# A graph message layer on one core: one of 124 edge groups is summed from SBUF instead of being scattered

## The chip, the cores and the metric

The kernel runs on one core of a Trainium2 chip. The metric is the time of one execution on the device in microseconds (us). A core has TensorE (PE, matmuls, with weight loads shown apart as PEld), VectorE (DVE), ScalarE (ACT), GpSimd (POOL) and SyncE (SP), each with its own instruction stream, and 16 DMA engines that all of them start transfers on. SBUF is the on-chip memory with 128 partitions, PSUM the memory that matmuls write to.

## The reference

There are 6250 nodes with 64 features and 206250 edges, sorted in the reference by destination. For each edge the features of one end (`col`) and the 64 edge attributes go through a layer with ReLU; the results are averaged over the edges of each node (`row`); two more layers, a residual and a layer norm follow per node. Everything is fp32.

```python
msg = jnp.concatenate([src_node_features[col], edge_attr], axis=1)
h = jax.nn.relu(msg @ W1a.T + b1a)          # 206250 x 128
h = h @ W1b.T + b1b
sums = jax.ops.segment_sum(h, row, num_segments=n_nodes)
counts = jax.ops.segment_sum(ones, row, num_segments=n_nodes)
agg = sums / jnp.maximum(counts, 1.0)[:, None]
z = jax.nn.relu(jnp.concatenate([x, agg], axis=1) @ W2a.T + b2a)
z = z @ W2b.T + b2b
out = layernorm(x + jnp.concatenate([z, x], axis=1) @ Wr.T + br)
```

The node that an edge is summed into (`row`, called src in the kernel) is random over all nodes; the node that it reads (`col`, dst in the kernel) rises along the list of edges.

## The kernel before

**Tiles, groups, bins.** Edges are padded to 206336 = 1612 tiles of 128. 13 tiles are a group (1664 edges); the 124 groups are taken in an order shuffled by a fixed step. Nodes are cut into 49 bins of 128. The second layer of the messages is applied after the mean, so what is summed per edge is the ReLU output, 128 numbers and a one for the count.

**Scatter and sum.** Edges of one bin lie anywhere in the list. So the kernel sorts rows by bin through DRAM: each group's 1664 rows (128 numbers, the one, and the node's place in its bin: 520 bytes) are written by 13 indirect DMAs on POOL, 128 rows each, to the next free slots of their bins (L959). Later the rows of a bin are read back in tiles of 128 (L1008, SP), DVE compares the place of each row with a ramp 0 to 127 to make a one-hot matrix per tile (L1037), and PE multiplies one-hot and rows, so that the rows of each node are added in PSUM (L1053). DVE adds the result into `part`, an SBUF array of all bins (L1109).

**Epochs and steps.** The groups are split in five epochs (`EPOCHS`, 82, 17, 14, 7 and 4 groups) that use three DRAM buffers in turn. Epoch 0 is read in steps: once 4, 8, 12, 16 and 18 tiles of every bin are surely full (`FULL`), those are read while later groups are still scattered; the last step of an epoch reads the rest up to a bound that no bin exceeds. A step's sums come in groups of up to 3 bins and 14 tiles ("sum groups"), spread evenly over the iterations of the next step and begun 4 iterations late (`LATE`). Nine buffers hold rows that were read (`READS`).

**The loop.** One iteration k handles group k (L1179 to L1263). In program order it

- starts the loads of group k+3 (`group`, L899): edge attributes into the upper half of an `rhs` buffer (L697, 416 KB), the places of the read nodes in a window of 64 nodes into its lower half (L914), and the 64 rows of the node table of that window into `mv` (L920). There are four `rhs` buffers (`EDGES`), so L697 waits until the matmuls of group k-1 have read theirs;
- counts bins for group k+1 on PE (`counts_of`, L852 and L853);
- computes the hidden layer of group k for tiles 0 to 9 (`hidden`, 128x128x128 matmuls at L952 in three parts; ACT applies the ReLU into an `orow` buffer, L953);
- makes the one-hot columns of group k+2 on DVE (`columns`, L932: 64x1664, in place over the places loaded by L914) and its bins and running counts (`bins_of`, L832, L833 and the scan L839);
- issues reads of rows for due sum groups as buffers are free (`issue`);
- does the due sum groups: `sum_next` runs the matmuls of one, makes the one-hots of the next (`mark`) and collects the one before. After the first, `slots` makes the row addresses of group k+1 (L869, L874). After the second (or after the only one), the last hidden part of group k is computed (tiles 10 to 12), and the scatter of group k is issued; a third sum group comes behind it.

The order on PE, ACT, DVE and SP is the order of the program (`manual_schedule`); an instruction that waits holds those behind it on its engine. POOL's scatters run in program order too; the eleventh of a group needs the ReLU of the last hidden part.

After the loop the last sums are done bin by bin together with the node layers and the layer norm (the tail). If the input doesn't fit the kernel's assumptions, a slower path is taken; it is not taken here.

Of the kernel before, what the change touches and what calls it, by code (L numbers as in the profile page):

```python
# [451 lines left out]
EPOCHS = (82, 17, 14, 7, 4)  # L452
# [4 lines left out]
BIG = 2.0**20  # L457
LATE = 4
# [5 lines left out]
ROWS, EDGES, READS = 5, 4, 9  # L464
# [13 lines left out]
def fast_path(  # L478
# [40 lines left out]
    NGR = NT // NG  # L519
    REM = N - (NB - 1) * P  # L520
# [6 lines left out]
    assert NT % NG == 0 and NGR == sum(EPOCHS) and HEAD % BLK == 0 and sorted(order) == list(range(NGR))  # L527
# [100 lines left out]
    mvs = const.tile([P, MV, H], F32, name="mv")  # L628
    nc.scalar.dma_start(mvs[:D], w1aT[D:, None, :].to_broadcast([D, MV, H]))
    mv = [mvs[:, i, :] for i in range(MV)]  # L630
# [45 lines left out]
    with (  # L676
# [17 lines left out]


        def edges(g):
            nc.sync.dma_start(rhss[g % EDGES][:D, :], edgeT[:, g * NG * P : (g + 1) * NG * P])  # L697
# [201 lines left out]
        def group(g):  # L899

            rhs = rhss[g % EDGES]
            if g < NEAR:
                all_of = dst[g * NG * P : (g + 1) * NG * P].rearrange("(o e) -> o e", o=1)
                s = nc.sync.dma_start(rhs[D:, :].bitcast(I32), all_of.to_broadcast([WIN, NG * P]))
                edges(g)
                with tc.issue_after(s.ins):
                    w = nc.sync.value_load(win_i[0:1, g : g + 1], min_val=0, max_val=N - WIN)
                nc.sync.dma_start(near[:D, g, :], xT[:, bass.ds(w, WIN)])
                return rhs, None, mv[g % MV]
            edges(g)  # L910

            half = NG * P // 2
            rel = rhs[D:, :].bitcast(BF16).rearrange("p (h e) -> p h e", h=2)[:, :, half:]
            s = nc.sync.dma_start(  # L914
                rel, relt[g : g + 1, :].rearrange("o (h e) -> o h e", h=2).to_broadcast([WIN, 2, half])
            )
            with tc.issue_after(s.ins):
                w = nc.sync.value_load(win_i[0:1, g : g + 1], min_val=0, max_val=N - WIN)
            m = mv[g % MV]
            nc.sync.dma_start(m[D:, :], ytab[bass.ds(w, WIN), :])  # L920
            return rhs, rel, m
# [23 lines left out]
        def hidden(k, parts):  # L945
            orow = orows[k % ROWS]
# [136 lines left out]

        class Sums:
# [6 lines left out]

        issued, marked, totals = [], [], []

        def mark():

            if issued:
                g = issued.pop(0)
                g.oh = nodes_of(g.st, g.reads)
                marked.append(g)
# [11 lines left out]
        def sum_next():  # L1111
# [5 lines left out]
            summed(g.st, g.reads, g.oh, lambda b: g.ps[:, b - g.b0, :])  # L1117
# [7 lines left out]
        groups_at = [[] for _ in range(NGR + LATE)]  # L1125
        for st, after in zip(steps, steps[1:]):
            grs = groups_of(st)
            n = after.at - st.at
            for i in range(n):
                groups_at[st.at + LATE + i] = [(st, g) for g in grs[i * len(grs) // n : (i + 1) * len(grs) // n]]  # L1130
        to_issue = []

        def issue(k):

            while to_issue and sum(len(g.reads) for g in issued + marked) + len(to_issue[0][1]) <= READS:
                issued.append(Sums(k, *to_issue.pop(0)))
# [42 lines left out]
        for k, ep_ in enumerate(epoch_of):  # L1179

            if k + 3 < NGR:
                made[k + 3] = group(k + 3)
# [8 lines left out]
            if k + 1 < NGR:  # L1191
# [9 lines left out]
            if k + 2 < NGR:  # L1201
# [19 lines left out]
            if k == 4:  # L1221
# [17 lines left out]
                nc.vector.tensor_add(wrx_t[:D, :], wrx_t[:D, :], ident[:D, :D])  # L1239
            if 0 <= k - PRE < -(-NB // SUB):  # L1240
# [5 lines left out]
            for i in range(max(due, 1)):  # L1246
# [3 lines left out]
                if i == 0 and k + 1 < NGR:  # L1250
                    slots(k + 1, counts)
                if i == min(1, max(due, 1) - 1):
                    if k > 0:
                        hidden(k, ((10, 3),))
                    made.pop(k)
                    scatter(ep_, k)
# [7 lines left out]
        for k in range(NGR, NGR + LATE):  # L1264
# [10 lines left out]
        with tc.tile_pool(name="nw", bufs=3) as nw:  # L1275
# [68 lines left out]
            for i in range(n_last + 5):  # L1344
                issue(NGR)
# [4 lines left out]
                issue(NGR)  # L1350
# [85 lines left out]
```

## Time and profile before

| | |
|---|---|
| median of 3 runs | 2570.15 us (2557.39 to 2579.05) |
| profiled execution | 2561.73 us, span 2559.9 us |
| granted TensorE clock, mean | 0.715 |
| busy: PE, PEld, DVE, ACT, POOL | 57%, 50%, 46%, 13%, 60% |
| scatters (L959) | 1612 of 958 ns, first at 14.6, last ends at 2434 |
| hidden matmuls (L952) | 3224 records, 642.8 us busy |
| sum matmuls (L1053) | 4006 records, 614.2 us busy |
| edge loads (L697, L914, L920) | 124 groups, 416 KB + 208 KB + window |

The profile is of one execution, by the hardware's profiler. An fp32 matmul leaves two records, so 2003 tiles were summed. "Idle before" an instruction is the time its engine stood still, with what ended it: "DMA rhs<-relt" is the landing of that transfer, "issue" means that the engine waited for nothing the profile shows, "remote" that the event came from a core or queue that the profile doesn't know. SPq and POOLq are instructions by which an engine starts a transfer. Groups are numbered in the order in which they are handled; "block k" are the 13 scatters of group k.

### The profile page before, as it was taken

Reading aid. Unit: us, or ns where it says so; the run is one execution under the profiler, and the core shown is the slowest. Engines: PE = TensorE matmul, PEld = TensorE weight load, DVE = VectorE, ACT = ScalarE, POOL = GpSimd, SP = SyncE. Lnnn points to the kernel's source line nnn. Section 1 sums busy time; section 2 is a strip of 40 time slices with the busy share of each in tenths; the row PEclk is TensorE's granted clock in tenths of the full one; section 3 lists DMA queues with packets and bytes.
Section 4 is the critical chain, followed back from the end, with each engine's and each line's share of the span. In section 5 each row is a group of like instructions: output and inputs, shape, how many; then the busy total and the mean of one; then the engine's idle time right before and its main releaser. Section 6 shows DMA issues by size and latency. Waiting matters only on the chain. (4 is left out here: it accounts for less than half of the span.)

```text
span 2559.9 us, 25031 instructions
## 1 busy us (share of the span) xinstructions
PE 1455.2 (57%) x8253; PEld 1270.7 (50%) x8253; DVE 1184.9 (46%) x1993; ACT 326.1 (13%) x807; POOL 1547.4 (60%) x1629
## 2 busy tenths in 40 slices
PE   4555543345555554545655566665666665666796
PEld 3444442344444444434544455555555564566695
DVE  5233334233343443533444345465555454555587
ACT  1111111111111010101101011111001010100106
POOL 5566666666666666666666665656666666666600
PEclk7656666666776776767676677776776776777899
DMA  7467635544434444434444455644545554555581
GB/s 163 142 224 239 194 116 165 179 116 116 135 115 122 133 120 120 127 106 134 123 133 119 128 153 150 170 131 142 155 139 153 154 145 148 158 167 171 162 258 38
DMA packets 198839, 375.23 MB, mean 147 GB/s; under 512 B 47105, under 2 KB 114036, under 8 KB 198572
## 3 DMA queue, kind: packets, MB, share of 16 engines
q1 hardware_dynamic: 121370, 223.70, 31.7%
q0 software_dynamic: 51584, 107.40, 13.2%
q10 hardware_dynamic: 25746, 42.45, 5.0%
q8 instruction: 67, 1.10, 0.2%
q14 instruction: 72, 0.59, 0.1%
HBM read 221.77 MB, written 151.59 MB: 146 GB/s over the span
## 5 line engine op out<-in xcount | busy, mean ns | idle before, releaser
L959 POOL DMA_INDIRECT rows<-orow,rowidx x1612 | 1544.9, 958 | 886.2 <-issue 472.9
L952 PE MATMUL h_ps<-mv,rhs 128*128 128x128 f32 x3224 | 642.8, 351 | 457.0 <-issue 313.5
L952 PEld LDWEIGHTS h_ps<-mv,rhs 128*128 128x128 f32 x3224 | 579.0, 260 | 532.9 <-issue 371.1
L1053 PE MATMUL sum_ps<-rt,oh 128*128 128x129 f32 x4006 | 614.2, 309 | 266.2 <-issue 224.9
L1053 PEld LDWEIGHTS sum_ps<-rt,oh 128*128 128x128 f32 x4006 | 572.7, 223 | 295.1 <-issue 249.4
L953 ACT ACTIVATE orow<-h_ps 128x512 f32<-128x512 f32 x496 | 247.8, 518 | 2046.4 <-remote 1228.3
L1037 DVE TENSOR_TENSOR oh<-ramp,rt 128x512 f32<-128x512 f32 (+3 forms) x213 | 145.6, 703 | 562.4 <-DMA rt<-rows 361.9
L932 DVE TENSOR_TENSOR rhs<-rhs,ramp 64x1664 f32<-64x1664 bf16 x116 | 219.5, 1892 | 30.4 <-DMA rhs<-relt 16.8
L1109 DVE TENSOR_TENSOR part<-part,sum_ps 128x258 f32<-128x258 f32 (+2 forms) x183 | 86.2, 472 | 273.5 <-remote 186.1
L839 DVE TENSOR_TENSOR_SCAN had<-ramp,bins 128x700 bf16<-128x700 bf16 x124 | 200.3, 1615 | 4.2
L852 PE MATMUL cnt_ps<-had,one_w 128*128 128x350 bf16 x248 | 101.4, 411 | 176.6 <-issue 101.3
L1037 DVE TENSOR_TENSOR oh<-ramp,node 128x512 f32<-128x512 f32 (+3 forms) x237 | 187.4, 791 | 8.0
L869 DVE TENSOR_REDUCE row<-cnt_ps 128x14 f32<-128x700 f32 x124 | 109.1, 880 | 52.4 <-PE cnt_ps L853 24.3
L853 PEld LDWEIGHTS <-before_w 128*128 128x128 bf16 x248 | 28.9, 117 | 201.1 <-issue 188.9
L1034 DVE SCALAR_TENSOR_TENSOR node<-unused,rt 128x4 f32<-128x4 bf16 (+3 forms) x237 | 37.9, 160 | 195.1 <-DMA rt<-rows 118.4
L853 PE MATMUL cnt_ps<-bins,before_w 128*128 128x325 bf16 x248 | 103.2, 419 | 31.2 <-issue 31.2
L833 DVE TENSOR_TENSOR bins<-ramp,hi 128x650 bf16<-128x650 f32 x124 | 108.2, 873 | 0.0
L1158 DVE TENSOR_SCALAR zT<-h_ps 128x512 f32<-128x512 f32 (+1 forms) x13 | 8.6, 661 | 140.3 <-remote 73.0
L852 PEld LDWEIGHTS <-one_w 128*128 128x128 bf16 x248 | 30.6, 123 | 59.9 <-issue 49.3
L1153 PE MATMUL h_ps<-zT,w2x_t 65*128 65x512 f32 (+1 forms) x26 | 22.2, 952 | 57.8 <-ACT orow L953 55.9
L1162 PE MATMUL h_ps<-nwzz_t,zT 128*128 128x64 f32 x98 | 22.3, 402 | 46.1 <-DVE zT L1158 43.2
L832 DVE TENSOR_TENSOR bins<-had,ramp 128x50 bf16<-128x50 bf16 x119 | 44.1, 370 | 2.7
(112 smaller groups left out, 390.9 us busy)
## 6 DMA issues: line engine op xcount, KB each, us to landing
rt<-rows SPq DMA_DIRECT2D x242, 260.0 KB
rhs<-in_edgeT SPq DMA_DIRECT2D x124, 416.0 KB
rt<-rows SPq DMA_DIRECT2D x106, 390.0 KB
rows<-orow,rowidx POOLq DMA_INDIRECT x1612
rhs<-relt SPq DMA_DIRECT2D x116, 208.0 KB
rows<-padrow ACTq DMA_DIRECT2D x4, 4680.0 KB
rows<-padrow ACTq DMA_DIRECT2D x8, 2340.0 KB
rt<-rows SPq DMA_DIRECT2D x48, 325.0 KB
```

The costliest lines, as they stand in the source:

```text
L833: nc.vector.tensor_tensor(by_bin[:, :, 1:], ramp[:, : 2 * HALF, None].to_broadcast([P, 2 * HALF, BLK]), hi[:, None, c0 : c0 + BLK].to_broa ...
L839: nc.vector.tensor_tensor_scan(had, on, oh, 0.0, op0=ALU.mult, op1=ALU.add)
L852: nc.tensor.matmul(v, one_w, had[:, b, :], start=True, stop=False)
L853: nc.tensor.matmul(v[:, :, :BLK], before_w, oh[:, b, 1:], start=False, stop=True)
L869: nc.vector.tensor_reduce(row, v.rearrange("p i b t -> p t i b"), axis=mybir.AxisListType.XY, op=ALU.max)
L932: nc.vector.tensor_tensor(rhs[D:, :].rearrange("p (h e) -> p h e", h=2), rel, in_win[D:, :, None].to_broadcast([WIN, 2, NG * P // 2]), op= ...
L952: nc.tensor.matmul(ps[:, j, :], rhs[:, c * P : (c + 1) * P], m, start=True, stop=True)
L953: nc.scalar.activation(orow[:, k0 : k0 + n, :H], ps[:, :n, :], AF.Relu)
L959: s = nc.gpsimd.indirect_dma_start(out=ep_.rows, out_offset=bass.IndirectOffsetOnAxis(ap=rowidx[:, t : t + 1], axis=0), in_=orow[:, j, :], ...
L1037: nc.vector.tensor_tensor(res[:, at_tile : at_tile + nb * n, :], ramp[:, None, :].to_broadcast([P, nb * n, P]), node[:, :, None].to_broadc ...
L1053: nc.tensor.matmul(of_bin(b), oh[:, at_tile, :], rt[:, j * n + t, : H + 1], start=t0 + t == st.lo[b], stop=t0 + t == st.hi[b] - 1,)
L1109: nc.vector.tensor_add(to, to, g.ps[:, : g.nb, :])
```

## The change

Group 123, the last, isn't scattered any more (`WHOLE = 1`); the loop runs over 123 groups (`NSC`) and the first epoch has 81. Group 123 is loaded at k = 10 into space lent from the read buffers and a fifth `mv` buffer, its columns are made at k = 13 and its hidden layer at k = 14, into an SBUF buffer of its own (`wrow`, 128x13x129). It is then summed bin by bin: each of 49 items subtracts 128 b from the node numbers, makes a one-hot of all 13 tiles for bin b in one operation (rows of other bins get none), multiplies the 13 tiles and adds the result into `part`. The items stand among the other sum groups in iterations 40 to 116.

The edge buffers (`rhs`) are three instead of four. Because the load of group k+3 then overwrites the buffer of group k, its issue moves from the start of iteration k to behind the last hidden part of group k.

With 81 groups in epoch 0, the bound on a bin's tiles is 24, not 25: the last step of the epoch reads 6 tiles of each bin (one read) where it read 7 (two reads of 4 and 3).

```diff
--- before.py
+++ after.py
@@ -449,19 +449,21 @@
 NG = 13
 WIN = 64
 STEP = 77
-EPOCHS = (82, 17, 14, 7, 4)
+EPOCHS = (81, 17, 14, 7, 4)
 NEAR = 8
 Y_AHEAD = 32
 HEAD = 117
 FULL = (4, 8, 12, 16, 18)
 BIG = 2.0**20
+WHOLE = 1
+WHOLE_AT = 10
 LATE = 4
 BUFS = 3
 RD = 6
 SUMS, TILES = 3, 14
 SEG = 9
 PRE = 6
-ROWS, EDGES, READS = 5, 4, 9
+ROWS, EDGES, READS = 5, 3, 9
 SPREAD = 4.8
 EARLY = 14
 CLEAR = 4
@@ -517,6 +519,7 @@
     E = NT * P
     NB = N // P + 1
     NGR = NT // NG
+    NSC = NGR - WHOLE
     REM = N - (NB - 1) * P
     NE = len(EPOCHS)
     W = H + 2
@@ -524,7 +527,7 @@
     HALF = -(-NB // 2)
     T = BLK + 1
     order = order_of(NGR)
-    assert NT % NG == 0 and NGR == sum(EPOCHS) and HEAD % BLK == 0 and sorted(order) == list(range(NGR))
+    assert NT % NG == 0 and NGR == sum(EPOCHS) + WHOLE and HEAD % BLK == 0 and sorted(order) == list(range(NGR))
 
     class Epoch:
         pass
@@ -625,9 +628,9 @@
     nc.scalar.dma_start(w1x_t[:D, :], w1aT[:D])
     nc.scalar.dma_start(w1x_t[D:, :], b1a.rearrange("(o p) -> o p", o=1))
     MV = 4
-    mvs = const.tile([P, MV, H], F32, name="mv")
-    nc.scalar.dma_start(mvs[:D], w1aT[D:, None, :].to_broadcast([D, MV, H]))
-    mv = [mvs[:, i, :] for i in range(MV)]
+    mvs = const.tile([P, MV + 1, H], F32, name="mv")
+    nc.scalar.dma_start(mvs[:D], w1aT[D:, None, :].to_broadcast([D, MV + 1, H]))
+    mv = [mvs[:, i, :] for i in range(MV + 1)]
     zT = const.tile([P, NB * P], F32, name="zT")
 
     near = lent(2 * NT + NG * P * 3 // 2, NEAR * WIN).rearrange("p (g w) -> p g w", w=WIN)
@@ -692,9 +695,16 @@
             nc.gpsimd.memset(r[:, :, H], 1.0)
         rhss = [rp.tile([P, NG * P], F32, name=f"rhs{i}") for i in range(EDGES)]
 
+        def rhs_of(g):
+            return rhss[g % EDGES] if g < NSC else lent(0, NG * P)
+
+
+        wrows = [op.tile([P, BLK, H + 1], F32, name=f"wrow{i}") for i in range(WHOLE)]
+        for r in wrows:
+            nc.gpsimd.memset(r[:, :, H], 1.0)
 
         def edges(g):
-            nc.sync.dma_start(rhss[g % EDGES][:D, :], edgeT[:, g * NG * P : (g + 1) * NG * P])
+            nc.sync.dma_start(rhs_of(g)[:D, :], edgeT[:, g * NG * P : (g + 1) * NG * P])
 
         dst_i = lent(2 * NT, NG * P)[:NGR].bitcast(I32)
         rel = lent(2 * NT + NG * P, NG * P // 2)[:NGR].bitcast(BF16)
@@ -898,7 +908,7 @@
 
         def group(g):
 
-            rhs = rhss[g % EDGES]
+            rhs = rhs_of(g)
             if g < NEAR:
                 all_of = dst[g * NG * P : (g + 1) * NG * P].rearrange("(o e) -> o e", o=1)
                 s = nc.sync.dma_start(rhs[D:, :].bitcast(I32), all_of.to_broadcast([WIN, NG * P]))
@@ -916,7 +926,7 @@
             )
             with tc.issue_after(s.ins):
                 w = nc.sync.value_load(win_i[0:1, g : g + 1], min_val=0, max_val=N - WIN)
-            m = mv[g % MV]
+            m = mv[g % MV if g < NSC else MV]
             nc.sync.dma_start(m[D:, :], ytab[bass.ds(w, WIN), :])
             return rhs, rel, m
 
@@ -943,7 +953,7 @@
         made = {}
 
         def hidden(k, parts):
-            orow = orows[k % ROWS]
+            orow = orows[k % ROWS] if k < NSC else wrows[k - NSC]
             rhs, _, m = made[k]
             for k0, n in parts:
                 ps = hp.tile([P, SUB, H], F32, name="h_ps")
@@ -1081,6 +1091,32 @@
                 res[-1].append((b, nb, t0, n))
             return res
 
+        class Whole:
+
+
+            def __init__(self, i, b):
+                self.st, self.reads, self.i, self.b0, self.nb = None, [], i, b, 1
+
+            def one_hots(self):
+                node = nodep.tile([P, BLK], F32, name="node_w")
+                nc.vector.tensor_scalar(node, wsrc[self.i], float(self.b0 * P), None, op0=ALU.subtract)
+                res = ohp.tile([P, TILES, P], F32, name="oh")
+                nc.vector.tensor_tensor(
+                    res[:, :BLK, :],
+                    ramp[:, None, :].to_broadcast([P, BLK, P]),
+                    node[:, :, None].to_broadcast([P, BLK, P]),
+                    op=ALU.is_equal,
+                )
+                return res
+
+            def sums(self):
+                for j in range(BLK):
+                    nc.tensor.matmul(
+                        self.ps[:, 0, :], self.oh[:, j, :], wrows[self.i][:, j, :], start=j == 0, stop=j == BLK - 1
+                    )
+
+        wsrc = [const.tile([P, BLK], F32, name=f"wsrc{i}") for i in range(WHOLE)]
+
         class Sums:
 
 
@@ -1089,13 +1125,19 @@
                 self.b0 = reads[0][0]
                 self.nb = reads[-1][0] + reads[-1][1] - self.b0
 
+            def one_hots(self):
+                return nodes_of(self.st, self.reads)
+
+            def sums(self):
+                summed(self.st, self.reads, self.oh, lambda b: self.ps[:, b - self.b0, :])
+
         issued, marked, totals = [], [], []
 
         def mark():
 
             if issued:
                 g = issued.pop(0)
-                g.oh = nodes_of(g.st, g.reads)
+                g.oh = g.one_hots()
                 marked.append(g)
 
         def collect(n):
@@ -1114,7 +1156,7 @@
                 mark()
             g = marked.pop(0)
             g.ps = spp.tile([P, SUMS, H + 1], F32, name="sum_ps")
-            summed(g.st, g.reads, g.oh, lambda b: g.ps[:, b - g.b0, :])
+            g.sums()
             totals.append(g)
             mark()
             collect(1)
@@ -1122,18 +1164,24 @@
 
         epoch_of = [ep_ for ep_ in epochs for _ in range(ep_.end - ep_.first)]
 
-        groups_at = [[] for _ in range(NGR + LATE)]
+        groups_at = [[] for _ in range(NSC + LATE)]
         for st, after in zip(steps, steps[1:]):
             grs = groups_of(st)
             n = after.at - st.at
             for i in range(n):
                 groups_at[st.at + LATE + i] = [(st, g) for g in grs[i * len(grs) // n : (i + 1) * len(grs) // n]]
+
+        of_whole = [(Whole(i, b), []) for i in range(WHOLE) for b in range(NB)]
+        at_whole, n = steps[1].at + LATE, NSC - 6 - steps[1].at - LATE
+        for i in range(n):
+            groups_at[at_whole + i] += of_whole[i * len(of_whole) // n : (i + 1) * len(of_whole) // n]
         to_issue = []
 
         def issue(k):
 
             while to_issue and sum(len(g.reads) for g in issued + marked) + len(to_issue[0][1]) <= READS:
-                issued.append(Sums(k, *to_issue.pop(0)))
+                st, of = to_issue.pop(0)
+                issued.append(st if isinstance(st, Whole) else Sums(k, st, of))
 
 
         clears = {5 + 2 * i: (0, i) for i in range(CLEAR)}
@@ -1178,8 +1226,6 @@
         slots(0, counts)
         for k, ep_ in enumerate(epoch_of):
 
-            if k + 3 < NGR:
-                made[k + 3] = group(k + 3)
             due = len(issued) + len(marked) + len(to_issue)
             to_issue += groups_at[k]
             nc.scalar.copy(orows[k % ROWS][:, :, H + 1], lo[:, k * BLK : (k + 1) * BLK])
@@ -1188,7 +1234,7 @@
                 window(1)
                 columns(1)
                 ahead = bins_of(1)
-            if k + 1 < NGR:
+            if k + 1 < NSC:
                 counts = counts_of(*ahead)
             if k > 0:
                 hidden(k, ((0, 4), (4, 3), (7, 3)))
@@ -1198,7 +1244,7 @@
                 load_x()
                 load_dst()
 
-            if k + 2 < NGR:
+            if k + 2 < NSC:
                 columns(k + 2)
                 ahead = bins_of(k + 2)
             if k == NEAR - 5:
@@ -1237,6 +1283,18 @@
                 nc.vector.tensor_add(w2x_t[D:, :], w2x_t[D:, :], wps[D : D + 1, :H])
                 nc.vector.tensor_add(wrx_t[D:, :], wrx_t[D:, :], wps[D : D + 1, H:])
                 nc.vector.tensor_add(wrx_t[:D, :], wrx_t[:D, :], ident[:D, :D])
+            for i in range(WHOLE):
+                if k == WHOLE_AT + 6 * i:
+                    made[NSC + i] = group(NSC + i)
+                    c0 = (NSC + i) * BLK
+                    nc.vector.scalar_tensor_tensor(
+                        wsrc[i], hi[:, c0 : c0 + BLK], float(P), lo[:, c0 : c0 + BLK], op0=ALU.mult, op1=ALU.add
+                    )
+                if k == WHOLE_AT + 6 * i + 3:
+                    columns(NSC + i)
+                if k == WHOLE_AT + 6 * i + 4:
+                    hidden(NSC + i, ((0, 4), (4, 3), (7, 3), (10, 3)))
+                    made.pop(NSC + i)
             if 0 <= k - PRE < -(-NB // SUB):
                 nodes_ahead((k - PRE) * SUB)
             if k in clears:
@@ -1247,12 +1305,14 @@
                 if due > 0:
                     sum_next()
                     issue(k)
-                if i == 0 and k + 1 < NGR:
+                if i == 0 and k + 1 < NSC:
                     slots(k + 1, counts)
                 if i == min(1, max(due, 1) - 1):
                     if k > 0:
                         hidden(k, ((10, 3),))
                     made.pop(k)
+                    if k + 3 < NSC:
+                        made[k + 3] = group(k + 3)
                     scatter(ep_, k)
             if due == 0:
                 collect(0)
@@ -1261,7 +1321,7 @@
             if k == NEAR - 4:
                 y_rows(Y_AHEAD, NB)
                 places_in_windows()
-        for k in range(NGR, NGR + LATE):
+        for k in range(NSC, NSC + LATE):
             to_issue += groups_at[k]
             issue(k)
             while issued or marked:
@@ -1342,12 +1402,12 @@
             to_issue += [(last, g) for g in groups_of(last)]
             n_last, on_way = len(to_issue), []
             for i in range(n_last + 5):
-                issue(NGR)
+                issue(NSC)
                 if i < n_last:
                     on_way.append(Nodes(sum_next()))
                 else:
                     collect(0)
-                issue(NGR)
+                issue(NSC)
                 for lag, stage in enumerate(("means", "turned", "layer", "residual", "written"), 1):
                     if 0 <= i - lag < n_last:
                         getattr(on_way[i - lag], stage)()
```

## The prediction, made before the changed kernel had run

> **What bounds the kernel now.** I read the page's span and costliest groups first, then the waits by engine, then a timeline of one iteration.
>
> ```profile
> span 2559.9 us, 25031 instructions
> PE 1455.2 (57%) x8253; PEld 1270.7 (50%) x8253; DVE 1184.9 (46%) x1993; ACT 326.1 (13%) x807; POOL 1547.4 (60%) x1629
> ...
> L959 POOL DMA_INDIRECT rows<-orow,rowidx x1612 | 1544.9, 958 | 886.2 <-issue 472.9
> ...
> L1053 PE MATMUL sum_ps<-rt,oh 128*128 128x129 f32 x4006 | 614.2, 309 | 266.2 <-issue 224.9
> ...
> L932 DVE TENSOR_TENSOR rhs<-rhs,ramp 64x1664 f32<-64x1664 bf16 x116 | 219.5, 1892 | 30.4 <-DMA rhs<-relt 16.8
> ```
>
> No engine is full. POOL is nearest: a group's 13 scatters take 13 x (0.96 + 0.30 issue) = 16.4 us, while the groups follow each other at 19 to 20 us from the first scatter (14.6) to the last (ends 2434). The missing 3 us is one pause per group, in the waits:
>
> ```profile
> ACT orow L953 <- remote: 1228.3, 122, 24.8
> ...
> DVE oh L1037 <- DMA rt<-rows: 361.9, 59, 24.6
> ...
> POOL rows L959 <- ACT orow L1185: 234.2, 57, 9.4
> ```
>
> ACT waits 1228 us for nothing the profile shows, and POOL waits for ACT. The timeline of block 92 (start, length, engine, instruction, idle before it) shows how:
>
> ```profile
> 1816.38 1.89 DVE L932 TENSOR_TENSOR rhs<-rhs,ramp 64x1664 f32<-64x1664 bf16 x1
> ...
> 1824.29 0.48 SPq L697 DMA_DIRECT2D rhs<-in_edgeT  x1
> 1824.35 0.49 ACT L953 ACTIVATE orow<-h_ps 128x384 f32<-128x384 f32 x1 [15.74 <-remote]
> ...
> 1825.12 0.96 POOL L959 DMA_INDIRECT rows<-orow,rowidx  x1 [3.30 <-ACT orow L1185]
> ...
> 1826.33 7.93 PE L1053 MATMUL sum_ps<-rt,oh 128*128 128x129 f32 x56
> ...
> 1835.58 1.89 DVE L932 TENSOR_TENSOR rhs<-rhs,ramp 64x1664 f32<-64x1664 bf16 x1
> ...
> 1837.23 0.37 PE L952 MATMUL h_ps<-mv,rhs 128*128 128x128 f32 x1 [1.13 <-issue]
> ...
> 1841.45 0.37 PE L952 MATMUL h_ps<-mv,rhs 128*128 128x128 f32 x1 [1.79 <-issue]
> ...
> 1843.81 0.49 SPq L697 DMA_DIRECT2D rhs<-in_edgeT  x1
> 1843.88 0.49 ACT L953 ACTIVATE orow<-h_ps 128x384 f32<-128x384 f32 x1 [16.75 <-remote]
> ...
> 1844.64 0.96 POOL L959 DMA_INDIRECT rows<-orow,rowidx  x1 [3.43 <-ACT orow L1185]
> ```
>
> POOL restarts at 1825.12, runs 13 scatters, stops at 1841.2. PE runs 56 sum records in 7.93 us (0.14 each), and from 1834 starts one instruction per 0.7 us. The last hidden part (three tiles, six records) is done on PE at 1837.6; its relu runs only at 1843.88, 2.7 us after POOL has stopped, and POOL restarts 0.8 us later. This is the reading that decides: **POOL waits for a relu that comes about 2.5 us after POOL's own stop, whether PE was ready 6 us earlier or just then.** Where PE is ready by that release, an iteration costs 16.4 + 3 us. Over the whole trace, PE has 63 such slow stretches (733 us). They begin after 111 to 150 PE instructions since POOL's restart in all but one, and that is 7.8 us after it in some and 18.7 us in others: a count, more than a time. PE that begins a sum late has lost little, then: it still has its fast instructions.
>
> **What goes.** Block 123's 13 scatters: one period of the last stretch, where the starts of blocks 117 to 123 stand 20.3 us apart: -20.3. The last step of epoch 0 becomes 6 tiles a bin in one read instead of 7 in two: 48 reads, 48 tiles and one one-hot operation each less; none ends a wait by itself; counted in the tiles below.
>
> **What comes.** 49 sums of 13 tiles: 637 matmuls (1274 records), net of the 48 tiles 1178 records. At 614.2/4006 = 0.153 us that is 180 us of PE over 83 iterations. On DVE, a one-hot of 128x1664: 512, 384 and 768 columns take 0.69, 0.55 and 0.96, so by slope about 1.9, and L932 with as many columns takes 1.89. With the subtraction (nearest L1034, 0.15 to 0.17) and the add into part (128x258 takes 0.41, so under that; 0.3) 2.4 us, 49 times = 116 us. All of it lies beside POOL's scatters unless it moves the release. What more tiles do to a period is read from stretches of before that had as many (starts of blocks, tiles per iteration from the step sizes):
>
> - blocks 24 to 40: 12 tiles, 18.95 us; 40 to 74: 12 tiles, 19.19
> - 74 to 85: 24 tiles, 19.95
> - 85 to 102: 21 on average, 19.94, with two long pauses; 102 to 117: 20.9, 19.46
> - 117 to 123: 34.9 tiles, 20.30
>
> After the change, 40 to 74 has 19.9 tiles: 34 x (19.46 - 19.19) = +9. 74 to 85 has 33.8: 11 x (20.30 - 19.95) = +4. 85 to 102 has 25.7 (before it alternated 14 and 28): 17 x 0 to 0.4, taken +3. 102 to 117 has 30.3: between 19.95 and 20.30, so 15 x 0.67 = +10. 117 to 123 the same. Together +26. The whole group's own load, columns (1.9) and 13 hidden matmuls at k = 10 to 14: +3, one longer pause (bounds 0 and 5).
>
> **What moves: the load.** L697 for group k+3 waited for the last hidden part of k-1; with three buffers it waits for that of k, and is written behind it. So a group's load is issued when the next group's was. It is 5.0 us from issue to data (1824.29 to 1829.4). In the trace a group's L932 starts 3.9 us (median) before the next group's load is through SP, 21 us before to 1.7 after in nine of ten. So L932 will nearly always wait, until 5 us after the release; behind it in DVE's order stand the bins scan (2.85), the next sum's one-hots, rowidx of the next group, and for the one-hots PE waits, with the last hidden part behind that sum where two or more are due (66 iterations; before 40). Worked out from the release: data 5.0, columns 6.9, bins 9.8, one-hots 10.5 (rows read) to 11.9 (whole): second sum from about 12 us. It needs 26 records and 6 of the hidden part, at 0.14 = 4.5 us: ready at 16.5, before the release at 19.5. If the slow pace catches it (24 to 29 PE instructions left at the release), those run at 0.07 to 0.2 us each: 2 to 6 us, of which such iterations already pay their share now, the period with 24 tiles being 19.95. Bounds 0 and +4 in 66 iterations, 0 to +264. I take 0, by the nearest row: in block 92 all 28 tiles and the hidden part came later than the release before and the pause stayed 3.4. Where three sums are due (29 iterations) DVE has 1.9 + 2.85 + 2.4 + two read sums (3.4) + two adds (0.8) + slots (1.2) = 12.6, and with 5 us of waiting 17.6 of 19.5 to 20.3: nearly full, +0.3 each = +9 (bounds 0 and 1.5). Rowidx is ready 3 us or more before its scatter. The first sum of an iteration has its one-hots from the iteration before.
>
> **Sum** against the profiled run (2561.73; span 2559.9): 2561.7 - 20.3 + 26 + 3 + 9 = 2579.4. The median of the runs, 2570.15, is 8.4 above that run, so 2588: +0.7%. About 1% is what a measurement of this kernel can tell from no change.
>
> The Trainium skill, "SBUF — State Buffer", section "Who interferes with whom", says that PE and ACT never wait on anyone. The rows above differ: PE falls to one instruction per 0.7 us and ACT stands 16.75 us while POOL scatters, by whatever way. By the rule the second sum would always be ready at 16.5 and the late load free: the sum stays at 2588, and only the bound of +264 falls. The same section says that tensor_scalar in a 2-port mode shuts GpSimd out, which speaks against the 49 new subtractions; by it they would cost at most 49 x 0.17 = 8 us, and no row shows a scatter stretched by DVE.
>
> **Rivals.**
> 1. *The late load sets the release* (the other side, slower). Place: the wait of L932 for relt, then one-hots, second sum, last hidden part, relu. It decides as soon as that part is ready later than 19.5 us after the last release. For it: the slow pace starts at 8 to 10 us in full iterations, before the second sum could begin, and pauses of 7.2, 7.9 and 9.4 us exist in blocks 75, 87 and 89. Against: block 92, and the count of fast instructions. Mildly, +1 us in 66 iterations: 2588 + 66 = 2654. Fully, +4 (3.5 to 6): 2588 + 264 = 2852.
> 2. *The added sums are free.* They run where PE waits anyway (43% of its span): 2561.7 - 20.3 + 8.4 = 2550. If the half as many reads also end the long pauses of blocks 87 and 89 (4 and 6 us over the usual) and that of 75 (4), 2536. Against: stretches with more tiles have longer periods today.
> 3. *The change doesn't do what it says.* Excluded: written out, the program has 13 scatters fewer and the sums where the diff puts them.
>
> **Numbers.** Forecast 0.50 (2560 to 2610, 0.08 of it beyond +1%); rival 1 mildly 0.25 (2600 to 2720), fully 0.12 (2720 to 2900); rival 2 0.13, of which 0.08 is more than 1% faster. So faster 0.08, same 0.42 + 0.05 = 0.47, slower 0.08 + 0.25 + 0.12 = 0.45. The range leaves out 0.08 below and 0.12 above: 2545 to 2720. The likeliest case's own is 2560 to 2610.
>
> **What would show it.** The columns operation (L932 before) waits for relt for hundreds of us instead of 16.8, yet POOL's idle time before its scatters stays near 886 us, less 4 for the missing block. L959 has 1599 instructions, L1053 and its whole twin together about 5184. Blocks 40 to 74 stand 19.4 to 19.6 apart. Wrong if the pauses of iterations with two or three sums due grow past 4.5 us: then rival 1, and the release has L932's wait in its chain.

## The result, and the profile after

The changed kernel takes 2610.37 us (median of 4 runs, 2601.06 to 2617.2), the kernel before 2572.61 us beside it. The ratio is **1.0153, 95% interval 1.0121 to 1.0186**: slower by some 39 us. The profiled execution took 2601.06 us with a span of 2599.1 us, 39.2 us more than the span before.

From the page of the changed kernel, the span and the groups that answer to those shown of before (the lines have moved by ten: L959 is L969, L1053 is L1063, L932 is L942; L1114 is new). Columns: instruction and count, busy us and mean ns of one, idle time of the engine before them and what ended most of it:

```profile
span 2599.1 us, 27457 instructions
...
L969 POOL DMA_INDIRECT rows<-orow,rowidx x1599 | 1532.9, 959 | 942.1 <-issue 458.3
L1063 PE MATMUL sum_ps<-rt,oh 128*128 128x129 f32 x3910 | 597.7, 314 | 338.5 <-issue 243.8
...
L942 DVE TENSOR_TENSOR rhs<-rhs,ramp 64x1664 f32<-64x1664 bf16 x115 | 217.5, 1891 | 962.7 <-DMA rhs<-relt 693.7
...
L1114 PE MATMUL sum_ps<-wrow,oh 128*128 128x129 f32 x1274 | 221.2, 341 | 176.1 <-issue 106.6
L1114 PEld LDWEIGHTS sum_ps<-wrow,oh 128*128 128x128 f32 x1274 | 209.5, 254 | 188.5 <-issue 121.5
```

The 13 scatters are gone (1599) and their busy time with them, 12 us less. But POOL's idle time before its scatters has grown from 886 to 942 us, where I had forecast no growth. DVE's wait for the edge load went from 16.8 to 693.7 us, as forecast. The two facts invite the conclusion that the late load made POOL wait. The experiments show that it didn't.

Where the time went by stretch, from the starts of the scatter blocks in the two traces:

| blocks | before, us a block | after, us a block | difference in all | forecast |
|---|---|---|---|---|
| 24 to 40 | 18.95 | 19.28 | +5 | 0 |
| 40 to 74 | 19.19 | 19.82 | +21 | +9 |
| 74 to 85 | 19.95 | 21.45 | +17 | +4 |
| 85 to 102 | 19.94 | 20.21 | +5 | +3 |
| 102 to 117 | 19.46 | 20.13 | +10 | +10 |

The rows add up to 58 us and the blocks before 24 to 1. From the start of block 117 to its last scatter the changed kernel takes 14.7 us less, with a block fewer there (the last six blocks of each take 118.8 us before and 123.5 after, where I had forecast no difference), and 4.8 less from there to the end: 39 in all.

Blocks in which POOL hardly pauses (under 1 us in all) were 11 of the 34 from 40 to 74 and are 5 now. Blocks with more than 5 us of pauses were 7 from block 24 on and are 17.

One of the 17 is block 66. From the timeline of the changed kernel (start, length, engine, instruction, idle time before it and what ended it):

```profile
1301.62 1.89 DVE L942 TENSOR_TENSOR rhs<-rhs,ramp 64x1664 f32<-64x1664 bf16 x1 [4.59 <-issue]
...
1308.73 1.23 PE L1114 MATMUL sum_ps<-wrow,oh 128*128 128x129 f32 x4 [5.75 <-DVE part L1151]
...
1310.48 0.37 PE L1114 MATMUL sum_ps<-wrow,oh 128*128 128x129 f32 x1 [0.53 <-issue]
...
1312.58 0.37 PE L1114 MATMUL sum_ps<-wrow,oh 128*128 128x129 f32 x1 [1.73 <-issue]
...
1314.71 0.38 PE L1114 MATMUL sum_ps<-wrow,oh 128*128 128x129 f32 x1 [1.76 <-issue]
...
1325.91 2.96 PE L1114 MATMUL sum_ps<-wrow,oh 128*128 128x129 f32 x13 [0.33 <-issue]
...
1328.66 1.49 PE L962 MATMUL h_ps<-mv,rhs 128*128 128x128 f32 x6
...
1330.24 0.49 ACT L963 ACTIVATE orow<-h_ps 128x384 f32<-128x384 f32 x1 [13.57 <-PE h_ps L962]
...
1331.01 0.95 POOL L969 DMA_INDIRECT rows<-orow,rowidx  x1 [8.97 <-ACT orow L1231]
```

An item of the whole group (26 records) starts at 1308.73. After four records PE starts its instructions 0.7 or 1.4 us apart. Half of the item is still to do when PE is fast again (13 records from 1325.91 in 2.96 us); then comes the last hidden part, its relu at 1330.24, and POOL has stood 9 us. Here the part that POOL waits for really is behind the sums. PE had waited 5.75 us for DVE before the item, and DVE had waited 4.59 us before its columns. What the timeline can't tell is whether the pause came because PE began the item late or because it had too much to issue; the run of the matmuls alone, below, bears on that.

### The profile page after: what moved, and what is told of

It reads as the page before. It is cut to its first block, busy times and chain, and to the rows that moved or that the text cites. A ratio compares the mean times of both kernels' runs of the same rounds, so it can differ in the third digit from the quotient of the medians.

```text
span 2599.1 us, 27457 instructions
## 1 busy us (share of the span) xinstructions
PE 1512.8 (58%) x9427; PEld 1384.3 (53%) x9427; DVE 1252.7 (48%) x2037; ACT 326.5 (13%) x806; POOL 1535.4 (59%) x1617
## 5 line engine op out<-in xcount | busy, mean ns | idle before, releaser
L969 POOL DMA_INDIRECT rows<-orow,rowidx x1599 | 1532.9, 959 | 942.1 <-issue 458.3
L1063 PE MATMUL sum_ps<-rt,oh 128*128 128x129 f32 x3910 | 597.7, 314 | 338.5 <-issue 243.8
L1063 PEld LDWEIGHTS sum_ps<-rt,oh 128*128 128x128 f32 x3910 | 563.6, 227 | 359.5 <-issue 258.7
L942 DVE TENSOR_TENSOR rhs<-rhs,ramp 64x1664 f32<-64x1664 bf16 x115 | 217.5, 1891 | 962.7 <-DMA rhs<-relt 693.7
L962 PE MATMUL h_ps<-mv,rhs 128*128 128x128 f32 x3198 | 524.9, 320 | 193.9 <-issue 107.1
L962 PEld LDWEIGHTS h_ps<-mv,rhs 128*128 128x128 f32 x3198 | 495.0, 234 | 227.7 <-issue 122.6
L1114 PE MATMUL sum_ps<-wrow,oh 128*128 128x129 f32 x1274 | 221.2, 341 | 176.1 <-issue 106.6
L1114 PEld LDWEIGHTS sum_ps<-wrow,oh 128*128 128x128 f32 x1274 | 209.5, 254 | 188.5 <-issue 121.5
L1151 DVE TENSOR_TENSOR part<-part,sum_ps 128x258 f32<-128x258 f32 (+2 forms) x232 | 99.8, 431 | 205.1 <-remote 170.0
L1047 DVE TENSOR_TENSOR oh<-ramp,node 128x768 f32<-128x768 f32 (+2 forms) x189 | 173.3, 917 | 6.3
L1104 DVE TENSOR_TENSOR oh<-ramp,node_w 128x1664 f32<-128x1664 f32 x49 | 92.7, 1891 | 1.7
L1210 PEld LDWEIGHTS h_ps<-nwzz_t,zT 128*128 128x128 f32 x98 | 21.9, 327 | 73.9 <-issue 64.9
```

The costliest lines, as they stand in the source:

```text
L942: nc.vector.tensor_tensor(rhs[D:, :].rearrange("p (h e) -> p h e", h=2), rel, in_win[D:, :, None].to_broadcast([WIN, 2, NG * P // 2]), op= ...
L962: nc.tensor.matmul(ps[:, j, :], rhs[:, c * P : (c + 1) * P], m, start=True, stop=True)
L969: s = nc.gpsimd.indirect_dma_start(out=ep_.rows, out_offset=bass.IndirectOffsetOnAxis(ap=rowidx[:, t : t + 1], axis=0), in_=orow[:, j, :], ...
L1047: nc.vector.tensor_tensor(res[:, at_tile : at_tile + nb * n, :], ramp[:, None, :].to_broadcast([P, nb * n, P]), node[:, :, None].to_broadc ...
L1063: nc.tensor.matmul(of_bin(b), oh[:, at_tile, :], rt[:, j * n + t, : H + 1], start=t0 + t == st.lo[b], stop=t0 + t == st.hi[b] - 1,)
L1114: nc.tensor.matmul(self.ps[:, 0, :], self.oh[:, j, :], wrows[self.i][:, j, :], start=j == 0, stop=j == BLK - 1)
```

## The experiments

The ratios below are each against the kernel before on the same chip, and the chips differ: the kernel before takes 2564.82 us beside the first four runs and some 2581 beside most others. The expectations in us were written for some 2570, so the ratios are what to read. Two theories at first. **A**: the late load lengthens the chain load, columns, bins, one-hots, second sum, relu, POOL. **B**: the load is hidden, and the added sums cost the time.

**The late load alone.**

```diff
-ROWS, EDGES, READS = 5, 4, 9
+ROWS, EDGES, READS = 5, 3, 9
...
-            if k + 3 < NGR:
-                made[k + 3] = group(k + 3)
             due = len(issued) + len(marked) + len(to_issue)
...
                     made.pop(k)
+                    if k + 3 < NGR:
+                        made[k + 3] = group(k + 3)
                     scatter(ep_, k)
```

> The kernel before with three edge buffers and the load of group k+3 issued behind the last hidden part of group k, and nothing else: all 124 groups are scattered, no sums are added. Theory A (the late load lengthens the chain load, columns, bins, one-hots, second sum, release): 25 to 45 us slower than before, 2595 to 2615, with the columns operation waiting hundreds of us for relt. Theory B (the added matmuls and one-hots cost the time, the load is hidden): within 8 us of before, though the columns operation waits as long.

Measured: 2562.83 us against 2564.82, ratio 0.9994 (0.9982 to 1.0007). From the page of this run, the scatters and the columns:

```profile
L959 POOL DMA_INDIRECT rows<-orow,rowidx x1612 | 1550.5, 962 | 875.3 <-issue 458.7
...
L932 DVE TENSOR_TENSOR rhs<-rhs,ramp 64x1664 f32<-64x1664 bf16 x116 | 219.4, 1892 | 1128.5 <-DMA rhs<-relt 922.3
```

DVE waits 922 us for the load, 230 more than in the changed kernel, and POOL's idle time is 875 us, no more than before (886). Theory A falls for the load by itself: here a wait of 900 us costs nothing.

**The sums with the load back in its place**, and its control, with four orow buffers to make room.

```diff
-ROWS, EDGES, READS = 5, 3, 9
+ROWS, EDGES, READS = 4, 4, 9
...
+            if k + 3 < NSC:
+                made[k + 3] = group(k + 3)
             due = len(issued) + len(marked) + len(to_issue)
...
-                    if k + 3 < NSC:
-                        made[k + 3] = group(k + 3)
                     scatter(ep_, k)
```

> The changed kernel with four edge buffers and the load back at the start of the iteration; the room comes from four orow buffers instead of five. Theory A: the saved scatter block shows, 2545 to 2565, faster than before. Theory B: as slow as the changed kernel, 2600 to 2617.

> The kernel before with four orow buffers instead of five, the control for the run with four edge buffers. Both theories: within 5 us of before, since POOL scatters a group one iteration after it is computed at the most. If it is slower, that much is taken off the other run.

Measured: 1.0111 (1.0079 to 1.0143), 2596.12 us, a little under the range of theory B and far above that of theory A, and 1.0007 (0.9987 to 1.0027) for the control. Four orow buffers cost nothing, and with the early load the change still costs 1.1%. This overlaps the 1.0153 of the changed kernel in its interval, so whether the late load costs 0 or 0.4% beside the sums stays open here; the run with the columns later on DVE bears on it.

**No sums.**

```diff
-        of_whole = [(Whole(i, b), []) for i in range(WHOLE) for b in range(NB)]
+        of_whole = []
```

> The changed kernel without the 49 sums of the whole group (so the rows of that group are missing in the means): 123 groups scattered, three buffers, late load, one-hots and matmuls of the items left out. Theory A: the late load remains, 2575 to 2595. Theory B: 20 us and more faster than before, 2540 to 2555.

Measured: 0.9958 (0.9943 to 0.9974), 11 us less than before. POOL's idle time is back where it was before the change:

```profile
L969 POOL DMA_INDIRECT rows<-orow,rowidx x1599 | 1537.8, 962 | 886.0 <-issue 461.4
```

So the 49 items cost 1.0153 - 0.9958 = 1.95%, some 50 us, and everything else in the change gains 11 us. Theory B holds in its direction. The gain is smaller than a block's period of 20.3 us, though. By stretch, blocks 74 to 85 take 20.64 us each here against 19.95 before, 8 us more in all; I come back to that in the last run.

What of an item costs? **C**: its hand-offs between DVE and PE (one-hots, sum, add, PSUM buffer free), which come one after the other where three groups are due. **D**: its instructions on PE.

**One matmul instead of 13; and 13 matmuls without one-hots and add.**

```diff
-                for j in range(BLK):
-                    nc.tensor.matmul(
-                        self.ps[:, 0, :], self.oh[:, j, :], wrows[self.i][:, j, :], start=j == 0, stop=j == BLK - 1
-                    )
+                nc.tensor.matmul(
+                    self.ps[:, 0, :], self.oh[:, 0, :], wrows[self.i][:, 0, :], start=True, stop=True
+                )
```

> The changed kernel with one matmul per item instead of 13 (so 12 of 13 tiles of the whole group are missing in the means); one-hots, the add into part and the order stay. Theory C (what costs is the hand-offs of an item between PE and DVE: one-hots, sum, add, PSUM buffer free again, with three groups in an iteration): 2590 to 2612, as slow as the changed kernel. Theory D (what costs is the number of PE instructions in an iteration): 2552 to 2568, like the run without items.

```diff
             def one_hots(self):
-                node = nodep.tile([P, BLK], F32, name="node_w")
...
-                return res
+                return ident
...
-                        self.ps[:, 0, :], self.oh[:, j, :], wrows[self.i][:, j, :], start=j == 0, stop=j == BLK - 1
+                        self.ps[:, 0, :], self.oh, wrows[self.i][:, j, :], start=j == 0, stop=j == BLK - 1
...
                 g = totals.pop(0)
+                if isinstance(g, Whole):
+                    continue
```

> The changed kernel whose items keep their 13 matmuls but multiply with the constant identity, make no one-hots and add nothing into part (so the rows of the whole group are missing in the means): PE's work without the hand-offs. Theory C: 2552 to 2572. Theory D: 2590 to 2612.

Measured: 0.9962 (0.9941 to 0.9983) with one matmul, 1.0167 (1.0134 to 1.0200) with the matmuls alone. From the pages, first the run with one matmul:

```profile
L969 POOL DMA_INDIRECT rows<-orow,rowidx x1599 | 1532.5, 958 | 906.2 <-issue 466.0
...
L1113 PE MATMUL sum_ps<-wrow,oh 128*128 128x129 f32 x98 | 29.7, 396 | 120.7 <-issue 77.1
```

and the run with the matmuls alone:

```profile
L969 POOL DMA_INDIRECT rows<-orow,rowidx x1599 | 1534.7, 960 | 955.6 <-issue 468.9
```

As ratios the two stand where D put them (the second a little over its range): one with no items at all (0.9958), the other with the whole change (1.0153). DVE's part (49 one-hots of 1.89 us, the subtractions, the adds) costs nothing that can be measured, though the intervals leave room for some 7 us; the matmuls and their weight loads cost the rest. The second run also answers the question of block 66: its items wait for no one-hots, and the cost is the same. 12 x 49 = 588 tiles make 2.05%, 53 us: 0.09 us per tile, while a tile is two matmul records and two weight loads.

**The columns later on DVE.**

```diff
-            if k + 2 < NSC:
-                columns(k + 2)
-                ahead = bins_of(k + 2)
...
                     slots(k + 1, counts)
+                if i == 0 and k + 2 < NSC:
+                    columns(k + 2)
+                    ahead = bins_of(k + 2)
```

> The changed kernel with the columns and bins of group k+2 behind the first sum of an iteration and the row addresses of group k+1, so that DVE makes the one-hots of the second sum before it waits for the load. If the late load costs something together with the items (the changed kernel against the run with four buffers, 0.4%): 2590 to 2602. If not: within 6 us of the changed kernel.

Measured: 1.0148 (1.0110 to 1.0186), as the changed kernel. The second sum's one-hots no longer stand behind the wait for the load, and nothing is gained. With the first run, this leaves little room for the late load: a part of the 0.4% by which the run with four buffers is lower isn't excluded, and no run shows it.

**One item per iteration, in the light iterations.**

```diff
-        at_whole, n = steps[1].at + LATE, NSC - 6 - steps[1].at - LATE
+        at_whole, n = steps[0].at + LATE + 3, 47
```

> The changed kernel with the 49 items in iterations 27 to 73, where one sum group is due in each, so that no iteration has three groups that had two before. Theory C: the long pauses at iterations 78 to 84 and after 102 shrink to those of the run without items; what is left is the lost cheap iterations, some 0.4 us in 47 iterations: 2565 to 2580. Theory D: PE's total is the same, 2590 to 2612.

Measured: 1.0068 (1.0044 to 1.0091), 2599.83 us against 2580.9. The number lies in D's range as written, but as a ratio between the two. Neither theory holds as I had put it: the same PE instructions cost 1.10% over the run without items here, and 1.95% where they were. So it is not their total alone. Blocks 74 to 85 fall from 21.45 to 20.23 us, 102 to 117 from 20.13 to 19.61, and 24 to 40 rise to 20.30; of the blocks 40 to 74 none is left without a pause. That fits an iteration with 25 tiles paying less for its second group than one with 37 for its third.

**Columns or instructions?** D1: PE's instructions cost by their number. D2: by the time for which PE streams.

```diff
-                        self.ps[:, 0, :], self.oh, wrows[self.i][:, j, :], start=j == 0, stop=j == BLK - 1
+                        self.ps[:, 0, :16], self.oh, wrows[self.i][:, j, :16], start=j == 0, stop=j == BLK - 1
```

> The run with the matmuls alone (identity, no one-hots, no add), with 16 columns per matmul instead of 129: as many PE instructions, an eighth of the columns streamed. It leaves out the rows of the whole group. Theory D1 (the number of PE instructions costs): 1.4% to 1.7% over before, as with 129 columns. Theory D2 (the time for which PE streams costs): between 0.4% under and 0.3% over before.

Measured: 1.0167 (1.0129 to 1.0206), to the last digit what 129 columns gave. The groups of the two runs, first the matmuls alone with 129 columns:

```profile
L1105 PE MATMUL sum_ps<-wrow,ident 128*128 128x129 f32 x1274 | 212.2, 322 | 146.8 <-issue 109.8
```

and with 16:

```profile
L1105 PEld LDWEIGHTS sum_ps<-wrow,ident 128*128 128x128 f32 x1274 | 216.6, 259 | 157.7 <-issue 98.5
L1105 PE MATMUL sum_ps<-wrow,ident 128*128 128x16 f32 x1274 | 214.9, 308 | 156.2 <-issue 97.4
```

The ratio is in D1's range, but the run doesn't divide D1 from D2 as cleanly as I had meant: with an eighth of the columns PE's busy time is the same (214.9 and 212.2 us), since the records lie as far apart as before. It does show that the cost goes with the pair of weight load and matmul, not with the columns that flow through it.

**Half the pairs.** The rows of the whole group as two bf16 numbers (value and remainder) side by side: one matmul and one weight load per tile, two adds. Then the same with one item per iteration.

```diff
-        wrows = [op.tile([P, BLK, H + 1], F32, name=f"wrow{i}") for i in range(WHOLE)]
+        wrows = [lent(NG * P, BLK * H).rearrange("p (b f) -> p b f", f=H)]
+        wbs = [op.tile([P, BLK, 2, H + 1], BF16, name=f"wb{i}") for i in range(WHOLE)]
...
+                    nc.vector.tensor_copy(wbs[i][:, :, 0, :H], wrows[i])
+                    nc.vector.tensor_tensor(wbs[i][:, :, 1, :H], wrows[i], wbs[i][:, :, 0, :H], op=ALU.subtract)
...
-                        self.ps[:, 0, :], self.oh[:, j, :], wrows[self.i][:, j, :], start=j == 0, stop=j == BLK - 1
+                        self.ps[:, :2, :], self.oh[:, j, :], wbs[self.i][:, j, :, :], start=j == 0, stop=j == BLK - 1
...
                     nc.vector.tensor_add(to, to, g.ps[:, : g.nb, :])
+                    if isinstance(g, Whole):
+                        nc.vector.tensor_add(to, to, g.ps[:, 1:2, :])
```

> The changed kernel with the rows of the whole group as a pair of bf16 numbers (value and remainder) side by side, 258 bf16 columns per matmul, one-hots in bf16, and two adds into part: two PE instructions per tile instead of four, and by the bf16 matmuls of the counts (325 to 350 columns in 0.31 to 0.50 us) about as much PE time, 0.25 to 0.4 us a tile against 2 x 0.17. D1: about half of the items' cost goes, 0.4% to 0.8% over before. D2: 1.3% to 1.8% over before.

> The same pair of bf16 numbers with the items one per iteration in iterations 27 to 73. If both help: the best of the versions, within 0.3% of before. If only the place helps: 0.5% to 0.8% over before. Below before is possible only if the items cost less than the 0.4% that the run without items gains.

Measured: 1.0017 (0.9999 to 1.0035) for the pair, 1.0005 (0.9978 to 1.0032) with one item per iteration. The pair's matmuls, from its page:

```profile
L1117 PE MATMUL sum_ps<-wb,oh 128*128 128x258 bf16 x637 | 123.5, 356 | 167.1 <-issue 95.0
...
L1117 PEld LDWEIGHTS <-oh 128*128 128x128 bf16 x637 | 78.2, 124 | 206.2 <-issue 139.4
```

Half of the records, and 123.5 us of matmul time instead of 221.2, less than I had assumed for D2. 0.17% over before lies under D1's range (0.4% to 0.8%) and far under D2's. The items' cost falls from 1.95% to 1.0017 - 0.9958 = 0.59%, by more than half; that would fit the last instructions of an iteration being the dear ones. Number and time on PE were both halved, so this run doesn't divide them either. The place gives little on top; both versions are level with before, neither beats it.

**The crowded step.** With 81 groups in epoch 0 its fifth step has three iterations, 82 to 84, for 17 sum groups where it had four: five or six groups in each, and in the changed kernel six or seven with the items. The last run takes the bf16 pair, spreads these sum groups over four iterations and keeps the items out of there.

```diff
-            n = after.at - st.at
+            n = max(4, after.at - st.at)
...
-                groups_at[st.at + LATE + i] = [(st, g) for g in grs[i * len(grs) // n : (i + 1) * len(grs) // n]]
+                groups_at[st.at + LATE + i] += [(st, g) for g in grs[i * len(grs) // n : (i + 1) * len(grs) // n]]
...
-        for i in range(n):
-            groups_at[at_whole + i] += of_whole[i * len(of_whole) // n : (i + 1) * len(of_whole) // n]
+        at = [k for k in range(at_whole, at_whole + n) if not 82 <= k < 86]
+        for i, k in enumerate(at):
+            groups_at[k] += of_whole[i * len(of_whole) // len(at) : (i + 1) * len(of_whole) // len(at)]
```

> The run with the pair of bf16 numbers, whose fifth step of epoch 0 (17 sum groups from iteration 82 on) is spread over four iterations, as before the change, instead of three, and whose items stay out of iterations 82 to 85. If the crowding there, a side effect of 81 groups, costs the excess of the pauses of blocks 83 to 85 (26.5 us together with the pair, 18.7 for blocks 83 to 86 before): 8 to 12 us less than with the pair, 0.996 to 0.999 of before, the first version with this change that is not slower. If it doesn't: 1.000 to 1.003.

Measured: 0.9967 (0.9954 to 0.9979), 2134.22 us against 2141.55. The ratio is where I had expected it, but for another reason, and the question isn't answered: this run was made on another chip, on which the kernel before takes 2141.55 us (10 runs, 2140.62 to 2142.03) where the chips of the other runs take 2565 to 2582. Its page and timeline:

```profile
span 2132.2 us, 26237 instructions
...
L971 POOL DMA_INDIRECT rows<-orow,rowidx x1599 | 1533.4, 959 | 507.6 <-issue 394.3
```

```profile
1508.00 0.96 POOL L971 DMA_INDIRECT rows<-orow,rowidx  x1 [0.30 <-DMA rows<-orow,rowidx]
1509.27 0.95 POOL L971 DMA_INDIRECT rows<-orow,rowidx  x1 [0.31 <-issue]
```

A scatter costs as much as everywhere (0.96 and 0.30), but the pauses are gone: from block 24 to the end a block takes 16.41 us, and no pause is over 0.6 us. The trace has no stretch in which PE starts one instruction per 0.7 us; those of the kernel before and of the pair without the spreading have 63 (733 us) and 29 (299 us). Here POOL bounds the loop, and PE's added work fits beside it; what it costs on this chip wasn't measured, since no run there leaves it out. Of the versions that sum every row, this is the only one that was measured to beat the kernel before, on this chip. Whether it does so on the others, and what the changed kernel itself does on this one, wasn't measured.

The slow stretches aren't themselves the measure of the cost. A like count (five or more starts on PE in a row that are 0.6 to 1.5 us apart, joined over breaks of up to 1.5 us) finds 66 of them (742 us) in the kernel before and only 32 (301 us) in the changed kernel, which is slower. What has grown is POOL's pauses: from block 24 on there are 87 of more than 1 us before (332 us in all) and 104 after (397 us).

## Why the prediction was right, and which step was not

The measured 2610.37 us lies inside 2545 to 2720, just above the likeliest case's own range (2560 to 2610). That case said 2588, 0.7% over before, and the time is 1.53% over. That the wide range held is partly luck: it reaches that far because of a rival that isn't what happened, and the errors of single terms took some of each other back. Of the signs, the wait for relt and the counts (1599, 5184) came as named; POOL's idle time and the distance of blocks 40 to 74 (19.82 us, not 19.4 to 19.6) didn't. The sign of being wrong came too, in pauses of up to 11.5 us, but it pointed at rival 1, which the runs don't bear out. By its steps:

- **POOL waits for a relu that comes about 2.5 us after its own stop**: right, and the ground of all that follows. It fits 922 us of DVE waiting for a load that cost nothing.
- **The late load, taken at 0 with a bound of 264 us**: right. 0.9994 alone. Rival 1, late load on the path, was the case to which I gave 0.37; the measured time reaches the range of its mild form (2600 to 2720), but no run shows its mechanism; beside the sums up to some 0.4% of it isn't excluded.
- **DVE nearly full where three groups are due, +9**: wrong by its size: one matmul per item gives 0.9962, no items at all 0.9958, so no cost is seen, within some 7 us.
- **The added sums, +26**: this is the step that failed. They cost 50 us (1.95%); the runs with one matmul and with the matmuls alone lie 53 us apart. I had read the price of more tiles from stretches of before with as many tiles on average: 19.46 us a block with 20.9 tiles, 20.30 with 34.9. But the mean of a stretch isn't what a block pays. From 40 to 74 the 12-tile blocks had pauses of some 4.6, 3.7 and 0.1 us in turn; with 25 tiles in more than half of the blocks the 0.1 mostly goes, and single pauses of 5 to 12 us come, 11 of the 17 where a third group is due, the others in one of two iterations with two groups that follow each other. That those full iterations run PE out of time is read from the trace and fits the run with one item in each light iteration (1.0068); it wasn't shown by itself. I had even named the mechanism ("24 to 29 PE instructions left at the release") and priced it at 2 to 6 us, and then took it as already paid because the 24-tile stretch showed 19.95 us. (The 83 iterations over which the prediction spreads the sums are 77, from 40 to 116; no term rests on it.)
- **Blocks 117 to 123 "the same"**: the last six blocks take 4.7 us more than before, a part of the 50.
- **One scatter block less, -20.3**: the change without its sums gained 11 us. I had counted the tiles that the shorter first epoch removes and overlooked that it takes one of four iterations from the fifth step. Blocks 74 to 85 without items take 8 us more than before. That the crowding is the cause fits the pauses (11.2 and 7.9 us in blocks 84 and 85 of that run) and wasn't shown, since the run meant for it fell on the other chip.

Together: -11 (in which the whole group's own load is contained) + 50 = +39 us against a forecast of -20.3 + 26 + 3 + 9 = +18. The 50 is the measured total less the run without items, so this sum had to come out; the 53 of the two runs is the check on it.

"SBUF — State Buffer" of the Trainium skill, section "Who interferes with whom", says that PE and ACT never wait on anyone. It says so of the ports of SBUF, and I had read it as a rule on PE's pace. As such it doesn't hold here: PE's added instructions cost 50 us, and the kernel before has slow stretches of 733 us. Whether a port has a part in them no run shows. On the chip of the last run PE has no slow stretch, and nothing in that trace is against the page.

## What to carry to other kernels

A wait of hundreds of microseconds in the profile can be free and busy matmuls on an engine that is 57% full can be dear: ask what the waiting engine holds back at the moment when the bound one is released. Price added work at the iterations that get most of it, not by the mean of a stretch with as much work. And when a list is made one shorter, look at what is divided among its parts: a step that loses one of four iterations has a third more to do in each.

## What the runs showed of the hardware that was not expected

- While POOL issues its indirect DMAs, PE can fall to one instruction per 0.7 us, mostly after its first 110 to 150 since POOL's restart (66 times before, 32 times after the change by the count above), on the chips on which the kernel takes 2565 to 2582 us. On another chip the same kernel takes 2141.55 us, and the last run's variant of it shows no such stretch. What differs between the chips the traces don't tell; the granted clock is higher on that one, too (0.76 for the kernel before, where it is 0.71 to 0.72 on the others).
- An fp32 matmul of 16 columns with its weight load of 128 columns took about as long on PE as one of 129 (308 and 322 ns a record, 214.9 and 212.2 us in all).
- POOL's scatter stayed at 958 to 962 ns in every run, with and without the 49 subtractions on DVE, so the mean shows no sign that these held it up.
